# Order edges around the four token scatters of a sequence, with a landing wait for each of the four

## The chip, the cores and the metric

The kernel runs on one core of a Trainium2 chip. A core has five engines, each with its own instruction stream: TensorE (PE in the profile, with its weight loads as PEld), VectorE (DVE), ScalarE (ACT), GpSimd (POOL) and SyncE (SP), which here only starts DMAs. An engine takes its instructions in the order of its stream and waits on semaphores where one needs what another engine or a DMA has to deliver. The metric is the device time of one execution in microseconds (us), as a median over several runs; lower is better.

## The reference

Two transformer layers over 16 sequences of 512 tokens of width 128, each part followed by a layernorm:

```python
x = _layernorm(x + _L0_attn_ref(x, ...), axis=-1)   # prefix sums over the tokens, 16 heads
x = _layernorm(x + _L0_ffn_ref(x, ...), axis=-1)    # 8 experts, the best one of each token
x = _layernorm(x + _L1_attn_ref(x, ...), axis=-1)   # softmax attention with a position bias
x = _layernorm(x + _L1_ffn_ref(x, ...), axis=-1)    # a shared expert, and the best of 8
```

What matters here are the two mixtures. Each token goes through one expert of eight, picked by the largest logit:

```python
logits = tokens @ Wr + br
expert = jnp.argmax(jax.nn.softmax(logits, axis=-1), axis=-1)
...
out = jnp.take_along_axis(y, expert[:, None, None], axis=1)[:, 0, :]
```

## The kernel before

The sequences are handled in six chunks of 2, 3, 4, 4, 2 and 1 (`CHUNKS`, L31). Layer 0 of the next chunk is woven between the attention of layer 1 of the present one and the mixture of layer 1 of the chunk before, so that all engines have work of several kinds.

A mixture works on lists. `route` (L576) finds the expert of every token of the chunk and gives each token a row number, `place`, in a list in DRAM that is sorted by expert; each slot of 128 rows belongs to one expert, whose row numbers in the weight table are in `rows`. `scatter` (L694) then sends the tokens of one sequence to their rows with four indirect DMAs on GpSimd, one for each 128 tokens (`send`, L703). There are 32 such sequences in the two layers, so 128 scatters of 64 KB. `slots` (L743) reads the list back four slots at a time: SyncE fetches the tokens (`fetch_tokens`, L755, tile `xq`), GpSimd gathers the weights of each slot (`fetch`, L770, tile `ws`), TensorE transposes the tokens (`pts`, L783) and multiplies (`ph` L1012 in layer 0, `pg` and `pu` L1385 in layer 1, `py` L808), and the results go back to DRAM. `gather` (L721) fetches each token's result with four indirect DMAs per sequence (tile `yg`); its first waits for the last of the sequence before. All indirect DMAs have the line of the helper `indirect`, L678.

GpSimd has other work too: in the attention of layer 0 (`tile0`, L884) the product `self` (L913) and a DMA that adds one row, `carry`, to `ev` (L920), before the prefix sums `cum` (L929); two small instructions `rs` in every layernorm (L520, L521); the scaled tokens `xs_m` of layer 1's mixture (L1334). Around these stand on TensorE `pv` (L894), whose product with `ex` is `ev` on VectorE (L907), the sums `ce` (L845, L847), `po` (L952) and `y` (L960). In layer 1's attention `s` (L1127, L1134), its maxima `tops` (L1149), their transposes `pm` (L1162), `st` (L1190), `p` (L1205 and L1211) and `av` (L1220) follow one another; SyncE moves rows into `qk_pad` between them (L1111, L1175).

The order of all this is computed ahead. Every piece of work is an `op` with an engine, a cost, a delay, what it reads and writes, and a due time. `Plan.order` (L106) plays the engines through in time: on each engine the able op that is due first starts, if its buffers are free. The op of the four scatters has the cost 5.1 us on GpSimd and a delay of 2.5 us. The result is one list over all engines. The ops are emitted in that order, and at the end (L1589) every instruction gets an edge without a semaphore, "NoSync", to the one emitted before it. Such an edge only asks that the second is not placed before the first when the streams of the engines are laid out; on the chip nothing waits for it.

In `send`, a scatter has edges of two other kinds. `awaits` adds edges with a semaphore: to the DMA that clears the list and to the fetches that read the list two chunks ago. And since all scatters write one DRAM tensor, the framework would draw an edge with a semaphore from each to the earlier ones; for the second to fourth of a sequence `declare_no_dep` takes out the edges to every scatter of the chunk sent so far, and for the first it is not called.

Of the kernel before, what the change touches and what calls it, by code (L numbers as in the profile page):

```python
# [20 lines left out]
NT = N // P  # L21
# [47 lines left out]
class Plan:  # L69
# [8 lines left out]
    def op(self, engine, cost, emit, reads=(), writes=(), delay=None):  # L78
        if delay is None:
            delay = (0.25, 0.12, 0.15, 0.15, 3.4)[engine]  # L80
        o = Op(len(self.ops), self.due, engine, cost, delay, emit)
        self.ops.append(o)
        before = set()
        for k in reads:
            if k in self.last:
                before.add(self.last[k])
        for k in writes:
            if k in self.last:
                before.add(self.last[k])
            before.update(self.readers.get(k, ()))  # L90
        for k in reads:
            self.readers.setdefault(k, []).append(o)
        for k in writes:
            self.last[k], self.readers[k] = o, []
        before.discard(o)
        for b in before:
            b.then.append(o)
        o.waits = len(before)
        for k in (*reads, *writes):
            buf = k[0] if isinstance(k, tuple) else k  # L100
            if isinstance(buf, Buf) and buf not in o.bufs:
                o.bufs.append(buf)
                buf.left += 1
        return o
# [76 lines left out]
def block_kernel(ctx: ExitStack, tc: tile.TileContext, d, out: bass.AP):  # L181
    nc = tc.nc
# [43 lines left out]
    op = plan.op  # L226
    names, listed = {}, {}
    placed, fetched, zeroed, gathered = {}, {}, {}, {}

    def buf(kind, name):  # L230
        pool, shape, dtype, bufs = kinds[kind]
        return Buf(
            kind, lambda: pool.tile(shape, dtype, tag=kind, name=name, bufs=bufs)
        )
# [84 lines left out]
    def tok(ap):  # L319
        return ap.rearrange("p (t w) -> p t w", w=W)  # L320
# [356 lines left out]
    def indirect(out=None, to=None, in_=None, of=None):  # L677
        nc.gpsimd.indirect_dma_start(  # L678
            out, bass.IndirectOffsetOnAxis(to, 0) if to is not None else None,
            in_, bass.IndirectOffsetOnAxis(of, 0) if of is not None else None,  # L680
        )

    def last():
        return list(nc.cur_bb.bb.instructions)[-1]

    def awaits(inst, others):
        for other in others:
            tc.add_manual_dep(
                inst, other.name,
                mybir.DependencyInfo(mybir.DependencyClass.Sync, mybir.DependencyReason.DATA),  # L690
                reason="list of tokens",
            )

    def scatter(which, c, i, src, place, store):  # L694

        n = f"{which}_{c}"
        sent, taken = placed.setdefault(n, []), fetched.get(f"{which}_{c - 2}", [])
        before = [f"zeros{which}_{c % 2}"]  # L700
        before += [f"fetched{which}_{c - 2}_{s}" for s in range(0, SLOTS, 4)]

        def send():  # L703
            for t in range(NT):
                indirect(
                    out=store[0], to=place()[:, NT * i + t : NT * i + t + 1],
                    in_=tok(src())[:, t, :],
                )
                inst = last()
                if t:  # L710
                    for other in sent:
                        tc.declare_no_dep(inst, other, reason="rows of their own")
                awaits(inst, [zeroed[f"{which}_{c % 2}"], *taken])
                sent.append(inst)

        op(
            POOL, 5.1, send, reads=[src, place, *before, f"token{n}_{i - 1}"],
            writes=[f"token{n}_{i}"], delay=2.5,
        )
# [862 lines left out]
    order = plan.order()  # L1582
    block = nc.cur_bb.bb.instructions
    mark = len(block)
    for o in order:
        for made in o.makes:
            made.tile = made.make()
        o.emit()
    chain = [i for i in list(nc.cur_bb.bb.instructions)[mark:]]  # L1589
    for before, then in zip(chain, chain[1:]):  # L1590
        tc.add_manual_dep(
            then, before.name,
            mybir.DependencyInfo(mybir.DependencyClass.NoSync, mybir.DependencyReason.DATA),
            reason="order",
        )


# [84 lines left out]
```

## Time and profile before

| | |
|---|---|
| median of three runs | 2499.63 us (2495.47 to 2499.99) |
| the profiled execution, its own time | 2567.31 us |
| its span, first to last instruction | 2564.4 us |
| granted TensorE clock in it | 0.938 |
| scatters (`tokens`, L678) | 128, median 0.97 us each |
| gathers of weights and of results (L678) | 212 in 207.6 us, 128 in 126.4 us |

All durations below are those of the profiled execution, which took 2.7% longer than the median of the runs. A line of a timeline has the start and the duration in us, engine, line, operation and tiles (written<-read), and in brackets the idle time of the engine before it with what ended it. "issue" there means that the engine waited for nothing that the profile shows. A line of the waits has who waited, for whom, the total in us, how often, and the longest. A line of the chain has start, duration, engine, tile and line. For a DMA that GpSimd starts, the duration is the engine's part alone, not the transfer.

### The profile page before, as it was taken

The page shows a single profiled execution, that of the slowest core. Times are in us where ns is not written, and L with a number is a line of the kernel's source. Part 1 is how long each engine was busy: PE and PEld are TensorE (multiplying, and loading weights), DVE is VectorE, ACT ScalarE, POOL GpSimd, SP SyncE. Part 2 cuts the span into 40 slices and gives each one's busy share as a digit, 9 for nine tenths or more (in the row PEclk, how much of TensorE's full clock was granted, in tenths as well). Part 3 has the DMA queues.
Part 4 walks back from the last instruction along what each step waited for, and adds up shares of the span by engine and source line. Part 5 has one row for each costly group of instructions (what it writes and reads, how often), then busy time and mean ns, then how long its engine had stood idle before and what let it go on. Part 6 is the DMA issues. An engine that isn't in the chain of part 4 may idle for free.

```text
span 2564.4 us, 33958 instructions
## 1 busy us (share of the span) xinstructions
PE 2258.0 (88%) x12820; PEld 1125.6 (44%) x12820; DVE 1934.8 (75%) x3030; ACT 1000.6 (39%) x1336; POOL 731.2 (29%) x763
## 2 busy tenths in 40 slices
PE   5978889899997997899889988899999889998974
PEld 4556424344553443355434423454344235443443
DVE  5455787897786789777778798778887886789761
ACT  6323144533433543333335443334454333444330
POOL 1244322323223244312132343212213323223232
PEclk9999889999998998898989998999999899998886
DMA  7613113112011331211023411122223112332332
GB/s 179 196 37 101 29 51 90 42 32 75 16 44 52 99 99 30 62 54 41 10 55 102 113 39 46 40 68 70 54 63 90 52 41 74 113 104 62 90 102 88
DMA packets 152438, 179.96 MB, mean 70 GB/s; under 512 B 19332, under 2 KB 125444, under 8 KB 152276
## 3 DMA queue, kind: packets, MB, share of 16 engines
q1 hardware_dynamic: 125588, 84.27, 12.5%
q0 software_dynamic: 26688, 93.53, 12.2%
q8 instruction: 101, 1.65, 0.3%
q14 instruction: 61, 0.50, 0.1%
HBM read 127.67 MB, written 42.93 MB: 67 GB/s over the span
## 4 chain that ended last, share of the span: by engine, by line
PE 58%; DVE 26%; ACT 5%; issue 5%; DMA 2%; another core or an unknown queue 2%; POOL 1%; SPq 0%; DVEq 0%; POOLq 0%; ACTq 0%
PE st L1190 9%; DVE p L1205 9%; PE av L1220 7%; PE s L1127 5%; DVE tops L1149 5%; PE y L960 4%; PE cum L929 4%; PE pv L894 4%; PE s L1134 3%; PE py L808 3%; ACT p L1211 2%; PE po L952 2%; PE pg L1385 2%; DVE o L941 2%
## 5 line engine op out<-in xcount | busy, mean ns | idle before, releaser
L1211 ACT ACTIVATE p<-p 128x1024 f32<-128x1024 f32 x512 | 539.4, 1058 | 539.0 <-DVE p L1205 480.8
L1205 DVE TENSOR_TENSOR p<-st,bias 128x1024 f32<-128x1024 f32 x512 | 606.0, 1216 | 126.1 <-PE st L1190 95.7
L1149 DVE TENSOR_REDUCE tops<-s 128x2 f32<-128x1024 f32 x512 | 604.7, 1215 | 72.5 <-PE s L1134 48.2
L1190 PE MATMUL st<-qk_pad 32*128 32x512 f32 x2048 | 385.2, 663 | 35.6 <-DVE p L1205 20.6
L678 POOL DMA_INDIRECT ws<-tab,rows x212 | 207.6, 979 | 678.9 <-PE py L808 317.8
L1127 PE MATMUL s<-bias,ident 128*128 128x512 bf16 x1024 | 329.4, 403 | 64.0 <-DVE p L1205 37.1
L1220 PE MATMUL av<-p,vaug 128*32 128x512 f32 x2048 | 291.6, 641 | 21.2 <-ACT p L1211 18.2
L913 POOL TENSOR_TENSOR self<-ev,own 128x1024 f32<-128x1024 f32 x64 | 122.6, 1917 | 514.5 <-DVE ev L907 283.7
L1134 PE MATMUL s<-qk_pad 32*128 32x512 bf16 x1024 | 207.0, 397 | 4.1 <-DMA qk_pad<-qk 4.0
L1190 PEld LDWEIGHTS st<-qk_pad 32*128 32x128 f32 x2048 | 113.5, 189 | 190.2 <-issue 70.5
L1127 PEld LDWEIGHTS <-ident 128*128 128x128 bf16 x1024 | 82.3, 99 | 234.6 <-issue 226.4
L678 POOL DMA_INDIRECT yg<-results,place x128 | 126.4, 988 | 141.2 <-issue 46.0
L1134 PEld LDWEIGHTS <-qk_pad 32*128 32x128 bf16 x1024 | 48.8, 91 | 244.2 <-issue 232.9
L929 PE MATMUL cum<-ev,tri 128*128 128x512 f32 x256 | 133.1, 647 | 10.2 <-DVE p L1205 5.1
L960 PEld LDWEIGHTS y<-ow,ot 128*128 128x128 f32 x1024 | 125.6, 197 | 32.8 <-issue 15.2
L960 PE MATMUL y<-ow,ot 128*128 128x128 f32 x1024 | 131.3, 283 | 3.2 <-ACT ot L955 2.6
L894 PE MATMUL pv<-vw,xt 128*128 128x512 f32 x256 | 130.1, 634 | 3.7 <-DVE p L1205 1.9
L941 DVE TENSOR_TENSOR o<-cum,gg 128x1024 f32<-128x1024 f32 x64 | 78.2, 1222 | 68.0 <-PE cum L929 53.2
L808 PEld LDWEIGHTS py<-ws,h 128*128 128x128 f32 x848 | 101.8, 195 | 36.2 <-DVE h L1309 14.4
L907 DVE TENSOR_TENSOR ev<-pv,ex 128x1024 f32<-128x1024 f32 x64 | 78.0, 1220 | 51.6 <-PE pv L894 45.3
L808 PE MATMUL py<-ws,h 128*128 128x128 f32 x848 | 111.2, 285 | 6.3 <-DVE h L1309 5.3
L952 PE MATMUL po<-ident,o 128*128 128x128 f32 x512 | 72.0, 286 | 36.7 <-DVE o L945 30.8
(189 smaller groups left out, 2757.0 us busy)
## 6 DMA issues: line engine op xcount, KB each, us to landing
xq<-tokens SPq DMA_DIRECT2D x44, 256.0 KB
results<-yq SPq DMA_DIRECT2D x44, 256.0 KB
qk_pad<-qk SPq DMA_DIRECT2D x256, 32.0 KB
slid<-line SPq DMA_DIRECT2D x16, 448.0 KB
tokens<-zero SPq DMA_DIRECT2D x4, 1472.0 KB
xt<-in_xt SPq DMA_DIRECT2D x16, 256.0 KB
x<-in_x SPq DMA_DIRECT2D x16, 256.0 KB
qk_pad<-qk SPq DMA_DIRECT2D x256, 16.0 KB
```

The costliest lines, as they stand in the source:

```text
L678: nc.gpsimd.indirect_dma_start(out, bass.IndirectOffsetOnAxis(to, 0) if to is not None else None, in_, bass.IndirectOffsetOnAxis(of, 0) if ...
L808: nc.tensor.matmul(py()[:, col(s)], h()[:, c, col(s)], ws[s]()[:, off + c * W : off + (c + 1) * W], start=(c == 0), stop=(c == 1),)
L894: nc.tensor.matmul(pv()[:, hf, :], xt()[:, col(t)], vw[:, hf * N : (hf + 1) * N], start=True, stop=True,)
L929: nc.tensor.matmul(cum()[:, hf, :], tri, ev()[:, hf, :], start=True, stop=True)
L960: nc.tensor.matmul(y()[:, :P], ot()[:, hf, col(c)], ow[:, 4 * hf + c, :], start=(hf == 0 and c == 0), stop=(hf == 1 and c == 3),)
L1127: nc.tensor.matmul(s()[:, i, :], ident16, bias16[:, 4 * g + 2 * jp + i, 2 * u + 1 : 2 * (u + N) : 2], start=True, stop=False,)
L1134: nc.tensor.matmul(s()[:, i, :], pad[r, 0, col(it)], pad[r, 1, :], start=False, stop=True,)
L1149: lambda s=s, jp=jp: nc.vector.tensor_reduce(tops[g % 2][:, it, 2 * jp : 2 * jp + 2], s(), AX.X, ALU.max, negate=True,),
L1190: nc.tensor.matmul(s[jp]()[:, i, :], pad[r, 1, col(jt)], pad[r, 0, :], start=True, stop=True,)
L1205: lambda jp=jp, h=h, pj=pj: nc.vector.tensor_tensor(pj(), s[jp](), bias[:, h : h + 2, u : u + N], ALU.add),
L1211: ACT, 1.0, lambda pj=pj: nc.scalar.activation(pj(), pj(), AF.Exp),
L1220: nc.tensor.matmul(acc()[32 * j : 32 * j + 32, :], va[:, jt, h * VW : h * VW + 32], p[j // 2]()[:, j % 2, :], start=(jt == 0), stop=(jt == ...
```

## The change

In `send`, the four scatters of a sequence are kept in a list of their own, `row`. `declare_no_dep` is called only between members of one row. Each of the four gets an edge with a semaphore to the four of the sequence before in the same chunk's list, in place of what the first alone had. The row is noted in `together` under the name of each of its members. At the end, the list of instructions is turned into a list of rows: a scatter's row stands as one entry, every other instruction is an entry of its own. The NoSync edges go from all members of an entry to all members of the next; none is drawn inside a row. Costs, delays and due times stay as they are, and so does the list that `Plan.order` makes.

```diff
     placed, fetched, zeroed, gathered = {}, {}, {}, {}
+    together = {}
...
         def send():
+            before, row = sent[-NT:], []
             for t in range(NT):
                 indirect(
                     out=store[0], to=place()[:, NT * i + t : NT * i + t + 1],
                     in_=tok(src())[:, t, :],
                 )
                 inst = last()
-                if t:
-                    for other in sent:
-                        tc.declare_no_dep(inst, other, reason="rows of their own")
-                awaits(inst, [zeroed[f"{which}_{c % 2}"], *taken])
-                sent.append(inst)
+                for other in row:
+                    tc.declare_no_dep(inst, other, reason="rows of their own")
+                awaits(inst, [zeroed[f"{which}_{c % 2}"], *taken, *before])
+                row.append(inst)
+            sent.extend(row)
+            for inst in row:
+                together[inst.name] = row
...
-    chain = [i for i in list(nc.cur_bb.bb.instructions)[mark:]]
+    chain = []
+    for i in list(nc.cur_bb.bb.instructions)[mark:]:
+        row = together.get(i.name, [i])
+        if i is row[0] or i.name == row[0].name:
+            chain.append(row)
     for before, then in zip(chain, chain[1:]):
-        tc.add_manual_dep(
-            then, before.name,
-            mybir.DependencyInfo(mybir.DependencyClass.NoSync, mybir.DependencyReason.DATA),
-            reason="order",
-        )
+        for a in before:
+            for b in then:
+                tc.add_manual_dep(
+                    b, a.name,
+                    mybir.DependencyInfo(
+                        mybir.DependencyClass.NoSync, mybir.DependencyReason.DATA
+                    ),
+                    reason="order",
+                )
```

## The prediction

> **What bounds the kernel now.** I read the page first: busy shares and the chain that ended last. Then POOL's timeline around the scatters (the first columns are start and duration in us, the bracket is the idle time before and what ended it), then who waits for whom, then the chain in the stretches where scatters run.
>
> ```profile
> PE 2258.0 (88%) x12820; PEld 1125.6 (44%) x12820; DVE 1934.8 (75%) x3030; ACT 1000.6 (39%) x1336; POOL 731.2 (29%) x763
> PE 58%; DVE 26%; ACT 5%; issue 5%; DMA 2%; another core or an unknown queue 2%; POOL 1%; SPq 0%; DVEq 0%; POOLq 0%; ACTq 0%
> ```
>
> TensorE and VectorE hand the end to each other. POOL, which the change concerns, is busy 29% and holds 1% of the chain. So the question is what a move on POOL does to the other two.
>
> ```profile
> 186.42 0.97 POOL L678 DMA_INDIRECT tokens<-x,place  x1 [0.30 <-issue]
> 187.69 0.96 POOL L678 DMA_INDIRECT tokens<-x,place  x1 [0.30 <-issue]
> 188.96 0.96 POOL L678 DMA_INDIRECT tokens<-x,place  x1 [0.30 <-issue]
> 190.23 0.97 POOL L678 DMA_INDIRECT tokens<-x,place  x1 [0.30 <-issue]
> 191.22 1.91 POOL L913 TENSOR_TENSOR self<-ev,own 128x1024 f32<-128x1024 f32 x1
> 193.44 0.95 POOL L920 DMA_DIRECT2D ev<-carry  x1 [0.31 <-POOL self L913]
> 194.69 1.03 POOL L678 DMA_INDIRECT tokens<-x,place  x1 [0.30 <-issue]
> ...
> POOL tokens L678 <- issue: 36.8, 121, 0.3
> ```
>
> This is the first chunk, two sequences, eight scatters from 182.26 on. Seven run in a row, one each 1.27 us, then come the product for `self` and the row add, then the eighth. One `send` emits its four scatters together, and the planner's list puts `self` and the row add between the two sequences' fours. So this issue order is not the list's: the edges between the four siblings, for which `declare_no_dep` is also called, are not in force, and the list falls apart at every sequence. And no scatter waits for a landing: the longest such gap is 0.3 us, plain issue.
>
> What a landing wait costs POOL is shown by the row gathers of the combine step, where the first of a sequence waits for the landing of the sequence before:
>
> ```profile
> 2321.47 0.94 POOL L678 DMA_INDIRECT yg<-results,place  x1 [0.30 <-issue]
> 2324.20 0.94 POOL L678 DMA_INDIRECT yg<-results,place  x1 [1.79 <-DMA yg<-results,place]
> ...
> 2500.31 0.97 POOL L678 DMA_INDIRECT tokens<-xs_m,place  x1 [0.30 <-issue]
> ...
> 2502.57 0.37 SPq L756 DMA_DIRECT2D xq<-tokens  x1
> ```
>
> 1.79 us instead of 0.30. The last two lines give the scatter's own landing: SyncE's fetch of the listed tokens starts 2.26 us after the last scatter's start.
>
> What stands on POOL behind the bursts:
>
> ```profile
> 398.43 0.99 POOL L678 DMA_INDIRECT ws<-tab,rows  x1 [45.10 <-PE st L1190]
> 832.53 1.90 POOL L913 TENSOR_TENSOR self<-ev,own 128x1024 f32<-128x1024 f32 x1 [17.46 <-DVE ev L907]
> 1358.14 0.99 POOL L678 DMA_INDIRECT ws<-tab,rows  x1 [4.98 <-PE py L808]
> 1864.11 0.23 POOL L520 TENSOR_SCALAR rs<-mv 128x4 f32<-128x4 f32 x1 [15.51 <-DVE mv L515]
> 2418.45 0.97 POOL L678 DMA_INDIRECT ws<-tab,rows  x1 [23.32 <-PE py L808]
> ```
>
> POOL idles long after nearly every burst; the shortest cover is 4.98 us, at 1353.
>
> **What the Trainium skill says.** "DMA: Bandwidth & Descriptors", section "Anatomy of one DMA — SWDGE (gpsimd) path": about 2.0 us plus bytes/436e3 per DMA, most of it completion, and a semaphore wait is held by the issuing sequencer. For a 64 KB scatter that makes an estimate of 2.15 us; the trace's 2.26 agrees. "Perfetto Trace Analysis", section "DMA Instruction — SWDGE (GPSIMD)": the reported end is that of descriptor generation. The trace agrees: 0.97 us reported, 2.26 to the landing. The first page, section "Two DMAs through the same engine are not ordered", asks for a wait only where bytes are shared; the scatters write rows of their own, so the new waits protect nothing that the time depends on.
>
> **The change part by part.**
>
> 1. The landing waits. 32 sequences scatter (16 in each layer), in 12 chunk lists; the first of a list has nothing before it, so 20 fours get a wait. Only the first of a four pays: the other three find it ended. Price of one: 1.79 − 0.30 = 1.49 us from the gather; from the scatter's landing 2.26 − 0.97 − 0.30 = 0.99 us. I take 1.3. In the planner's list 5 of the 20 have enough POOL work between (`self` with the row add, four weight gathers, or the layernorm's `rs`), 2 have one `xs_m` product (1.03 us, 0.3 left), 13 are bare: 13 × 1.3 + 0.6 = 17.5 us of added POOL idle (13.5 to 20). At most two bare ones fall in one burst, 2.6 us, against the covers above (45, 17, 29, 15, 23 us). Charged to the end: 0.
>
> 2. The restored order on POOL. Where the list has `self` and the row add between two fours (first chunk at 187, layer-1 lists at 581 and 2111), they go back before three (or six) scatters: 3 × 1.27 = 3.8 us earlier, 7.6 at 2111. Nobody waited for them: in the first chunk the chain runs over other work (below), at 581 the row add issued at 587.23 is first needed by `cum` at 594.26, at 2125.74 `cum` follows PE work without a gap. Gain 0; if they were waited for, up to 3.8 + 3.8 + 7.6 = 15 us.
> Later go: in layer 0's second chunk of four (1326 to 1353) the list puts eight scatters behind `rs`, which waits to 1349.25 for VectorE; today only two are there. After `rs` at 1350.8 now come 8 × 1.27 + 1.3 = 11.5 us, so POOL is free at 1362.2, and the weight gather of 1358.14 starts 4.1 us late. Its last packets, now at 1367.5, come near 1371.6; `ph` starts at 1371.17 and needs the fourth tile 1.5 us later. So it just fits (loss 0 to 4). The last token lands at about 1363.1, and SyncE, issuing attention rows until 1364.3, reaches the fetch after that: 1.2 us of slack. In layer 0's first chunk of four (784 to 815) three scatters go behind the weight gathers: the fetch at 818.03 moves by 3.8 us, and SyncE's next order is not due before 830.79. Cost 0.
>
> 3. The restored order elsewhere. Comparing the list with the issue order, PE differs in 5 places, DVE and ACT in one each, SyncE nowhere. Two matter in the chain. At 188.98 `ce` runs before `pv` though `ev` waits for `pv`:
>
> ```profile
> 188.98 0.17 PE ce L845 x2
> 189.15 0.63 PE ce L847 x6
> 189.78 2.68 PE pv L894 x4
> 192.46 0.02 issue
> 192.48 1.24 DVE ev L907
> ```
>
> With `pv` first the 0.80 us of `ce` fall into PE's idle time before `cum`: −0.8. At 360.30 three transposes `pm` (0.73 us) stand before `st`, for which DVE waits 1.60 us: −0.7. The other three places exchange works of under 1 us with PE busy before and after: 0 ± 0.5 each.
>
> 4. More instructions: a few semaphore reads on POOL, 17 ns each, covered as in 1. Buffers and semaphores may be handed out in another order where the order differed; the trace can't show it. I bound it at 4 us either way, since nearly every pool is full there and has one buffer to give, and take 0.
>
> Sum: −0.8 − 0.7 = −1.5 us on the profiled execution, whose own time is 2567.3 (span 2564.4); the runs shown have a median of 2499.6, 2.6% below it, which takes nothing noticeable off 1.5. Forecast: 2498.
>
> **Rivals.**
> A, slower: the stretch 1350 to 1372 is not covered. For it: the chain there really passes the token fetch (5.14 us from 1364.63 until `pts`), and the weights then move beside it. It decides from the point where the last weight tile lands after 1372.7, or the last token after 1364.3. Price: 4.1 us for the weights and about 1.5 for the fetch: 2505. Against it: both fit on paper.
> B, faster: `self` and the row add were late today, and what follows them moves up by the 15 us of part 2; half of that gives 2492, all of it 2485. Against it: the chain doesn't pass POOL in these places.
> C, it doesn't do what it says: the list is still not kept, only waits are added. Then part 1 alone, covered: 2499.6.
> All 17.5 us of waits on the path would give 2517; the covers speak against it, and I leave it outside.
>
> **How the numbers follow.** Likeliest 2498 with 0.48, its own range 2494 to 2503 from the 4 us of part 4. A 0.25, B 0.20, C 0.07. What can be told from no change is 0.2%, 5.0 us: 2494.6 to 2504.6. A and its neighbours give slower 0.25; B gives faster 0.22; the rest, same 0.53. The range reaches from B's half to beyond A by the 4 us of part 4: 2488 to 2509.
>
> **What would show it.** Four scatters of one sequence adjacent on POOL, `self` between the fours in the first chunk; 13 gaps of about 1.6 us (0.3 + 1.3) released by the DMA of `tokens`; POOL's busy time unchanged; `pv` before `ce` at 189; no new waits of `pts` or `ph`. I am wrong if the gaps are over 4 us, if `ph` near 1371 waits for `ws`, if SyncE's wait at the token fetch grows in front of attention rows, or if the time moves while these places do not.

## The result and the profile after

The changed kernel takes 2495.77 us (median of 20 runs, 2488.25 to 2503.71), the kernel before beside it 2501.77 (20 runs, 2495.47 to 2516.98). The ratio is 0.9972 with a 95% interval of 0.9959 to 0.9985: 0.28% less, some 7 us (the medians stand 6.0 apart). The forecast was 2498 and "no change"; the time lies in the range, and the gain is just above what can be told from none.

The profiled execution of after has 2503.2 us (span 2501.2). That of before had 2567.3 (span 2564.4), although the three runs listed with it took 2495 to 2500 and none of the twenty here more than 2517. So the two profiles stand 64 us apart where the runs stand 6 apart. Part of this document is about those 58 us, since the prediction read its places in the longer profile.

First the page of after, busy time and chain of waits:

```profile
PE 2242.6 (90%) x12820; PEld 1122.7 (45%) x12820; DVE 1936.2 (77%) x3030; ACT 1000.9 (40%) x1336; POOL 734.1 (29%) x763
...
PE 60%; DVE 25%; ACT 5%; issue 4%; DMA 3%; POOL 2%; SPq 0%; DVEq 0%; POOLq 0%; ACTq 0%
```

TensorE has 15 us less busy time for the same 12820 products (at a mean granted clock of 0.942 against 0.938), and the 2% of "another core or an unknown queue" are gone from the chain. GpSimd (POOL) does the same work as before, 734.1 us against 731.2.

GpSimd's timeline of after in the first chunk, with one landing wait of a later list (start and duration in us, in brackets the idle time before and what ended it), and its waits (total, times, longest):

```profile
187.14 1.02 POOL L679 DMA_INDIRECT tokens<-x,place  x1 [0.31 <-issue]
188.46 1.46 POOL L679 DMA_INDIRECT tokens<-x,place  x1 [0.30 <-issue]
190.22 0.97 POOL L679 DMA_INDIRECT tokens<-x,place  x1 [0.30 <-issue]
191.50 0.97 POOL L679 DMA_INDIRECT tokens<-x,place  x1 [0.30 <-issue]
192.48 1.92 POOL L917 TENSOR_TENSOR self<-ev,own 128x1024 f32<-128x1024 f32 x1
194.70 0.95 POOL L924 DMA_DIRECT2D ev<-carry  x1 [0.30 <-POOL self L917]
195.95 1.03 POOL L679 DMA_INDIRECT tokens<-x,place  x1 [0.30 <-issue]
...
347.37 0.97 POOL L679 DMA_INDIRECT tokens<-x,place  x1 [0.30 <-issue]
350.46 0.97 POOL L679 DMA_INDIRECT tokens<-x,place  x1 [2.12 <-DMA tokens<-x,place]
```

```profile
POOL tokens L679 <- issue: 37.0, 107, 2.5
...
POOL tokens L679 <- DMA tokens<-xs_m,place: 13.9, 10, 2.3
POOL tokens L679 <- DMA tokens<-x,place: 13.1, 6, 3.2
```

The change did what it says. The fours are adjacent, and `self` and the row add stand between two of them. The two named groups hold 16 idle times, 27.0 us in all, but three of these are the ordinary 0.3 us that stands in front of any scatter. The 13 others last 2.0 us on average, and two more, of 2.1 and 2.5 us, stand under "issue". So 15 scatters pause for a landing, 2.05 us each, where the prediction had 13 of 1.6. In front of all 128 scatters GpSimd idles 118.0 us, whatever it waits for, against 91.5 before.

### The profile page after: what moved, and what is told of

The parts are those of the page before. It is cut to its first block, busy times and chain, and to the rows that moved or that the text cites. A ratio compares the mean times of both kernels' runs of the same rounds, so it can differ in the third digit from the quotient of the medians.

```text
span 2501.2 us, 33949 instructions
## 1 busy us (share of the span) xinstructions
PE 2242.6 (90%) x12820; PEld 1122.7 (45%) x12820; DVE 1936.2 (77%) x3030; ACT 1000.9 (40%) x1336; POOL 734.1 (29%) x763
## 4 chain that ended last, share of the span: by engine, by line
PE 60%; DVE 25%; ACT 5%; issue 4%; DMA 3%; POOL 2%; SPq 0%; DVEq 0%; POOLq 0%; ACTq 0%
PE st L1194 9%; DVE p L1209 8%; PE av L1224 7%; PE s L1131 6%; DVE tops L1153 5%; PE y L964 4%; PE pv L898 4%; PE py L812 4%; PE cum L933 4%; PE s L1138 3%; PE po L956 2%; ACT p L1215 2%; PE pg L1389 2%; DVE o L945 2%; PE ph L1016 2%
## 5 line engine op out<-in xcount | busy, mean ns | idle before, releaser
L1194 PE MATMUL st<-qk_pad 32*128 32x512 f32 x2048 | 378.0, 662 | 25.2 <-DVE p L1209 20.7
```

Source lines behind the costliest of these rows:

```text
L1194: nc.tensor.matmul(s[jp]()[:, i, :], pad[r, 1, col(jt)], pad[r, 0, :], start=True, stop=True,)
```

## The experiments

They ran in three groups, each on a chip of its own with the kernel before beside it: e1 to e4 where before took 2572.3 us, e5 to e8 where it took 2502.2, e9 to e12 where it took 2504.2. That the same kernel takes 70 us more on one chip turned out to be half of the answer.

### Taking the change apart: e1 to e4

**e1** is the kernel before and **e4** the changed kernel, both unedited. **e2** has the changed edges and order without the landing waits:

```diff
-                for other in row:
+                for other in [*sent, *row]:
                     tc.declare_no_dep(inst, other, reason="rows of their own")
-                awaits(inst, [zeroed[f"{which}_{c % 2}"], *taken, *before])
+                awaits(inst, [zeroed[f"{which}_{c % 2}"], *taken])
```

**e3** has the waits without the order: the chain of before, and each scatter waits for the preceding four:

```diff
+            before, row = sent[-NT:], []
...
-                if t:
-                    for other in sent:
-                        tc.declare_no_dep(inst, other, reason="rows of their own")
-                awaits(inst, [zeroed[f"{which}_{c % 2}"], *taken])
-                sent.append(inst)
+                for other in row:
+                    tc.declare_no_dep(inst, other, reason="rows of their own")
+                awaits(inst, [zeroed[f"{which}_{c % 2}"], *taken, *before])
+                row.append(inst)
+            sent.extend(row)
```

TensorE, VectorE and ScalarE issue in e3 as in before. GpSimd differs at two places: once `rs`, and at the list of 2111 `self` with the row add, go out ahead of three scatters that stand before them in e1.

> The kernel before, unchanged. Theory N (the profiled execution of before was an odd one): a profile near the runs' median, 2495 to 2517 us, and VectorE's idle gaps in the scatter bursts (8.3 us at 804, 4.1 at 1039, 5.0 at 1346, 4.7 at 1595) are gone. Theory S (long runs of scatters that nothing holds back stall TensorE): the same gaps at the same places again, a profile several us above that of the changed kernel. Ratio 1.000 +- 0.001 in both.

> The changed kernel's issue order on all engines, but no scatter waits for the landing of an earlier one. Theory O (the restored order is what gains: pv before ce, st before the transposes, self earlier): the whole gain, ratio 0.997, VectorE's gaps in the bursts gone. Theory S (the landing waits gain, since they break the runs of scatters): no gain, 0.999 to 1.001, and gaps of 3 to 8 us at 800, 1040, 1345 and 1600 stay.

> The landing waits of the change, with the edges between neighbours as before: PE, DVE, ACT and SP keep the order of before, and three of four scatters of the next sequence still stand ahead of the last of the present one. Theory O: no gain, 0.999 to 1.001. Theory S: the gain, ratio 0.997 to 0.998, gaps in the bursts gone.

> The changed kernel, unchanged. All theories: ratio 0.996 to 0.9985, no gap of VectorE over 3 us in the bursts at 800, 1040, 1345 and 1600.

Measured against before on that chip: e1 0.9996 (0.9975 to 1.0016), e2 0.9935 (0.9910 to 0.9960), e3 0.9785 (0.9767 to 0.9803), e4 0.9801 (0.9779 to 0.9822). Here the change is worth 2%, and the waits, which the prediction priced as a cost to be hidden, bring all of it alone. Theory N falls, since before's profile comes out at 2573.5 again. The sizes were missed: e3 and e4 gain several times what was expected of them, and the order alone (e2) brings a third of the whole, more than theory O gave it and more than the nothing of theory S.

Where the time went is seen at one burst. GpSimd, TensorE and VectorE in e1, with the burst whose scatters begin at 1041.30 ("remote" is a releaser that the profile cannot name):

```profile
1048.99 0.96 POOL L678 DMA_INDIRECT tokens<-xs_m,place  x1 [0.30 <-issue]
1050.26 0.97 POOL L678 DMA_INDIRECT tokens<-xs_m,place  x1 [0.30 <-issue]
...
1047.67 0.62 PE L1127 MATMUL s<-bias,ident 128*128 128x512 bf16 x2
1048.23 0.39 PE L1134 MATMUL s<-qk_pad 32*128 32x512 bf16 x2
1048.55 1.06 PE L1220 MATMUL av<-p,vaug 128*32 128x512 f32 x8
1051.04 1.13 PE L1190 MATMUL st<-qk_pad 32*128 32x512 f32 x4 [1.42 <-issue]
1055.24 2.08 PE L1190 MATMUL st<-qk_pad 32*128 32x512 f32 x4 [3.08 <-issue]
...
1049.76 1.23 DVE L1149 TENSOR_REDUCE tops<-s 128x2 f32<-128x1024 f32 x1 [4.15 <-PE av L1220]
1053.96 1.22 DVE L1149 TENSOR_REDUCE tops<-s 128x2 f32<-128x1024 f32 x1 [2.98 <-remote]
1057.46 1.23 DVE L1149 TENSOR_REDUCE tops<-s 128x2 f32<-128x1024 f32 x1 [2.28 <-PE st L1190]
```

The same three reductions in e3:

```profile
1019.17 3.49 DVE L1150 TENSOR_REDUCE tops<-s 128x2 f32<-128x1024 f32 x3 [2.08 <-PE s L1135]
```

In e1 the last of the three `s` tiles was sent by TensorE at 1048.23, yet VectorE gets them at 1049.76, 1053.96 and 1057.46, one in four microseconds; TensorE in turn waits for what VectorE should have done, with gaps that the profile can only call "issue". TensorE's signals for these three tiles, which the trace keeps, are late as well: 1049.73, 1053.94 and 1057.44, where e9 (below), the same kernel on another chip, has 1016.09, 1017.01 and 1017.89. So the delay lies with TensorE or its signal, not with VectorE. In e3 the three follow each other without a gap. The row of granted clock has a dip to 0.5 for 10.2 us from 1052.78 on in e1 and none there in e3. It begins 3 us after the first late tile, so it does not start the stall; how much of the later delay it carries was not tried.

Matching VectorE's instructions of e1 one by one with those of e3 gives what each run of GpSimd's issues lost, from its start to 8 us after its end. The last column is the same between e9 and e10, that is on a chip where before takes 2504 us:

| run in e1, from | indirect transfers in a row | lost on e3 | e9 on e10 |
|---|---|---|---|
| 343.8 | 12 | 8.5 us | 1.1 us |
| 790.6 | 15 | 8.6 | −0.3 |
| 1036.1 | 16 | 8.9 | 0.1 |
| 1335.7 | 14 | 5.3 | −0.6 |
| 1590.3 | 15 | 9.7 | 0.0 |
| 2113.7 | 14 | 4.5 | 2.0 |
| 2392.1 | 12 | 2.6 | 2.8 |
| 37 runs of four weight gathers, sum | 4 each | −0.9 | 5.5 |

These seven hold 48 of the 61 us. The last two are weak evidence, since e9 loses 2 to 3 us on e10 there as well. Length alone does not decide it either: of two runs of eleven in e1 one loses nothing (from 181.8) and one 2.2 us (from 577.1), and one of eight (from 1851.1) loses 5.7. A check comes from the changed kernel. In e4 it still has one run of twelve, from 790.84 on, where four weight gathers follow four scatters and the next four follow these without a pause. Matched with e12, the same kernel on another chip, it loses 11.2 us there and at most 3.3 in any of its runs of eight. VectorE in e4, behind that run's start:

```profile
798.25 1.23 DVE L1153 TENSOR_REDUCE tops<-s 128x2 f32<-128x1024 f32 x1 [3.66 <-issue]
...
808.32 1.22 DVE L1209 TENSOR_TENSOR p<-st,bias 128x1024 f32<-128x1024 f32 x1 [6.03 <-remote]
```

These are gaps over 3 us, which were expected to be gone in e4. e3 has no run longer than eight.

So on this chip a run of a dozen and more indirect transfers, one each 1.27 us, can stall TensorE, in the burst shown from some 8 us after its first scatter on, and pauses of about 2 us between the fours prevent it. Theory S holds for this chip, as far as it names runs and pauses; its "no gain" for the order alone does not. The order shortens some runs too (the fourteen from 1335.7 on are two of eight in e2), so the gain of e2 is not clear of the stall.

### Pauses without waits, waits without pauses: e5 to e8

e5 fills a spare tile instead of waiting, e6 waits for landings long past, e7 waits in twos, and e8 is a measurement by itself. Against e2, the changed kernel, and the changed kernel:

```diff
+            for _ in before[:3]:
+                nc.gpsimd.memset(spare, 0.0)
             for t in range(NT):
```

```diff
-            before, row = sent[-NT:], []
+            before, row = sent[-2 * NT : -NT], []
...
-                for other in row:
+                for other in [*sent[-NT:], *row]:
```

```diff
-            before, row = sent[-NT:], []
+            before, row = sent[-2:], []
...
-                for other in row:
+                pair = row[t // 2 * 2 :]
+                if t == 2:
+                    before = row[:2]
+                for other in pair:
```

The core of e8, and its five parts:

```python
        for step in range(STEPS):
            s = ps.tile([P, N], F32, tag="s", name="s")
            nc.tensor.matmul(s, ident16, x16, start=True, stop=False)
            nc.tensor.matmul(s, ident16, x16, start=False, stop=True)
...
    parts = [
        lambda: send(0, False, False), lambda: send(1, True, False),
        lambda: send(2, False, True), fills, lambda: send(3, False, False),
    ]
```

> The order of the change without its landing waits, as in e2; instead GpSimd fills a spare tile three times (0.7 us each, some 2.1 us together) before each four that would have waited for the four before it: 60 fills, no scatter waits for a landing. The scatters are then broken up in fours as in the changed kernel, by work and not by a wait. Theory S, that a long run of scatters issued back to back stalls TensorE and that any pause of about 2 us ends it: the gain of the changed kernel comes back, a ratio of 0.978 to 0.984 where the changed kernel had 0.980 and order alone 0.9935; VectorE's gaps of 3 to 8 us in front of `tops`, `p` and `h` in the scatter stretches are gone. Rival W, that the wait for the landing itself is what helps (GpSimd idle, or the data in memory): no more than order alone, 0.991 to 0.996, with the gaps still there. Rival F, that GpSimd's fills slow VectorE: over 0.996.

> The changed kernel, but each four waits for the landing of the four before the preceding one, so for scatters issued 5 to 8 places earlier. At 1.27 us for an issue and 2.2 us to land these have landed when their turn comes, so the waits are there and are met, and scatters still go out back to back. Theory S: nothing of the landing waits' gain is left, the ratio is that of order alone, 0.991 to 0.996, the group `tokens <- DMA tokens` is under 3 us, and VectorE's gaps are those of e2. Rival W, that it is the waits as such (semaphores read, fewer scatters outstanding than the queue allows): 0.978 to 0.984.

> The changed kernel, but in twos: each two scatters wait for the landing of the two before them, so the pauses are more than twice as many (some 48 instead of 20, 80 to 100 us of GpSimd idle instead of 27) and no run is longer than two. Theory S: fours were short enough already, nothing more is gained, and the longer scatter stretches are mostly covered: 0.978 to 0.985. Rival G, that the stall grows from the first scatters on and fours still pay some of it: below 0.976. Rival C, that the longer stretches hold up `rs`, `self` and the weight gathers: over 0.987.

> The computation is left out: TensorE makes the same 128x512 tile from two bf16 products 720 times, VectorE reduces each one, and nothing on these two depends on GpSimd. Beside that GpSimd does five things, each begun on a result of VectorE 120 tiles after the last: 24 scatters of 128 rows of 512 bytes back to back; 24 where each four waits for the landing of the four before; 24 with three fills of a spare tile between fours; 48 fills; and 24 back to back again. Theory S: the tiles run at a steady pace of 0.6 to 0.9 us except in the first and the fifth part, where from 8 to 10 us after the first scatter on VectorE waits 2 to 5 us for a tile, until the run ends; the other three parts keep the pace. Rival K, that the stall needs something else of this kernel (weight gathers on the same queue, transfers of SyncE, transposes): the pace is the same in all five parts. Rival B, that any GpSimd work beside TensorE does it: the part with fills is slow too.

Measured: e5 0.9980 (0.9967 to 0.9994), e6 0.9941 (0.9921 to 0.9961), e7 1.0062 (1.0046 to 1.0078). The expectations were written for a chip like the first. On this one the stall does not occur: matched with the profile of after, e6 loses at most 1.6 us in any of its unbroken runs of 8 to 16. So e5 and e6 leave open whether a pause filled with work would have done as well as a wait. What they show is the other side, the price of pauses where nothing is won by them: none in e6, 15 in the changed kernel (0.9972), 20 filled ones in e5, and in e7 these:

```profile
POOL tokens L679 <- issue: 66.0, 93, 3.7
...
POOL tokens L679 <- DMA tokens<-xs_m,place: 35.2, 16, 3.8
POOL tokens L679 <- DMA tokens<-x,place: 26.9, 13, 2.6
```

In front of the scatters of e7 GpSimd idles 182 us, against 118 in the changed kernel and 91 in before. That costs e7 0.9% against the changed kernel and 1.2% against e6, which ran on the same chip: rival C of that run. The intervals of e5 and e6 do not meet either, so the filled pauses cost something there. Fours are affordable, twos are not.

e8, of which there is one execution, is level. Its page, VectorE's group (busy time and mean ns, then idle time in front) and the row of the granted clock:

```profile
PEclk9999999999999999999999999999999999999999
...
L261 DVE TENSOR_REDUCE top<-s 128x4 f32<-128x512 f32 x720 | 431.1, 672 | 1.9 <-PE s L259 1.8
```

720 tiles and 1.9 us of idle time in all, 24 scatters back to back or not. As the stall is absent on this chip from the whole kernel too, that does not say what else it needs.

### Where nothing stalls: e9 to e12

**e9** is before and **e12** the changed kernel, unedited, **e10** is the kernel of e3. **e11** restores the order of everything but the scatters: a second chain of edges runs past them, so TensorE, VectorE and ScalarE issue as in the changed kernel and GpSimd as in before.

```diff
+                row.add(inst.name)
...
-    for before, then in zip(chain, chain[1:]):
+    rest = [i for i in chain if i.name not in row]
+    for before, then in [*zip(chain, chain[1:]), *zip(rest, rest[1:])]:
```

> The kernel before once more, unchanged, for its profile: the profiled executions of before so far (2567.3 us, and e1 with 2575.3) both belong to the slow kind, while 41 timed executions beside e5 to e7 had a median of 2502.2. Theory T, two kinds of chips (or of places of the program in memory): where the times beside it are near 2500, the profiled span is near 2500 too, the long runs of scatters are there all the same, and VectorE's gaps of 3 to 8 us in front of `tops`, `p` and `h` behind them are missing; where the times are near 2570 the gaps are there. Rival: the profiler makes them, so that a profile near 2565 comes with times near 2500. Ratio 0.998 to 1.002.

> The neighbour edges of before, so its order on TensorE, VectorE and ScalarE, with each scatter waiting for the landing of the four before, as in e3. Theory T on a chip where before takes about 2500 us: no stall is there to be broken up, so the pauses can only cost: 1.000 to 1.006 (e6 without pauses stood at 0.9941, the changed kernel with 27 us of pauses at 0.9972, e7 with over 60 us at 1.0062, so about 0.003 for 27 us). Where before takes about 2570 us: 0.977 to 0.981, as in e3. Rival: the pauses cost nothing and e6, after and e7 differ for another reason: 0.998 to 1.000.

> No landing waits; the scatters stay where before has them, loose between each other, and GpSimd's whole order is that of before. Edges past the scatters hold the other instructions in the order written out, so TensorE (52 positions), VectorE (2) and ScalarE (3) issue as in the changed kernel. It splits part 3 of the prediction from part 2. Theory P, that the gain of order alone (0.9941 in e6, 0.9935 in e2) is TensorE's restored order: 0.992 to 0.996. Rival G, that it is GpSimd's restored order (the self term, the row addition and the weight gathers no longer pushed back by scatters): 0.998 to 1.001. The prediction's own sizes, 0 for GpSimd's order and 1.5 us for TensorE's, would give 0.9994.

> The changed kernel again, unchanged, on the chip of e9 to e11, so that the four add up: (order of the rest) and (GpSimd's order) and (waits). Where before takes about 2500 us: 0.996 to 0.999. Where it takes about 2570: 0.978 to 0.982.

Measured: e9 0.9989 (0.9973 to 1.0005), e10 0.9990 (0.9972 to 1.0009), e11 0.9978 (0.9967 to 0.9988), e12 0.9963 (0.9942 to 0.9985). The profile of e9 has a span of 2502.5 us, so the profiler does not make the 60 us on this chip. T holds: the stall belongs to the chip, or to something that differs between loads on it, and not to the program alone. e10 lies where its rival had it (the pauses cost nothing), e11 between its two theories. GpSimd in e9 issues runs as long as in e1 (the table above), and in the same burst as shown of e1 (here its sixteen issues go from 1004.7 to 1024.9) VectorE gets its three tiles like this:

```profile
1016.11 3.48 DVE L1149 TENSOR_REDUCE tops<-s 128x2 f32<-128x1024 f32 x3 [1.92 <-PE s L1134]
1020.08 1.23 DVE L1205 TENSOR_TENSOR p<-st,bias 128x1024 f32<-128x1024 f32 x1 [0.48 <-PE st L1190]
```

One more thing sets the profiles apart, and it tells which kind the one shown of before is. The traces keep the signals by which DMAs report that they have landed. There are 12487 of them in before and 12415 to 12905 in e1 to e4, but 16866 to 16949 in after, e5 to e7 and e9 to e12. A scatter has nearly all of its 16 in e9, and in e1 on average 5.9 in layer 0 and 3.8 in layer 1. So the profile shown of before has the mark of the chip of e1 to e4. Whether these signals are only missing from the record, or are held up on the chip together with TensorE, the runs do not tell.

The clean profile of before also shows what the order did. GpSimd, TensorE and VectorE in e9, then in e12, in the last layer-1 list:

```profile
2059.76 0.97 POOL L678 DMA_INDIRECT tokens<-xs_m,place  x1 [0.30 <-issue]
2060.76 1.91 POOL L913 TENSOR_TENSOR self<-ev,own 128x1024 f32<-128x1024 f32 x1
2062.97 0.95 POOL L920 DMA_DIRECT2D ev<-carry  x1 [0.30 <-POOL self L913]
...
2065.17 1.95 PE L929 MATMUL cum<-ev,tri 128*128 128x512 f32 x4 [2.83 <-DMA ev<-carry]
...
2067.16 1.22 DVE L941 TENSOR_TENSOR o<-cum,gg 128x1024 f32<-128x1024 f32 x1 [3.33 <-PE cum L929]
```

```profile
2053.07 1.91 POOL L917 TENSOR_TENSOR self<-ev,own 128x1024 f32<-128x1024 f32 x1
2055.28 0.95 POOL L924 DMA_DIRECT2D ev<-carry  x1 [0.30 <-POOL self L917]
...
2062.25 1.98 PE L933 MATMUL cum<-ev,tri 128*128 128x512 f32 x4
...
2064.27 1.23 DVE L945 TENSOR_TENSOR o<-cum,gg 128x1024 f32<-128x1024 f32 x1 [0.47 <-PE cum L933]
```

The two profiles stand at the same time here to within 0.1 us. In e9 the row add stands behind ten scatters and TensorE's cumulative sum waits 2.83 us for it. In e12 it goes out 7.7 us earlier, the wait is gone, and VectorE gets `cum` 2.9 us earlier. In e11, where GpSimd keeps the order of before, VectorE's gap at this place is 6.50 us.

And here is what the order and the waits cost, at the place of rival A. TensorE in e9, then in e12:

```profile
1329.61 0.66 PE L783 MATMUL pts<-ident,xq 128*128 128x128 f32 x4 [1.66 <-DMA xq<-tokens]
...
1331.56 3.00 PE L1012 MATMUL ph<-xqt,ws 128*128 128x128 f32 x16
...
1336.56 2.05 PE L808 MATMUL py<-ws,h 128*128 128x128 f32 x16
```

```profile
1330.69 1.12 PE L787 MATMUL pts<-ident,xq 128*128 128x128 f32 x4 [2.79 <-DMA xq<-tokens]
...
1333.13 3.78 PE L1016 MATMUL ph<-xqt,ws 128*128 128x128 f32 x16
...
1338.95 2.05 PE L812 MATMUL py<-ws,h 128*128 128x128 f32 x16
```

The last scatter in front starts at 1320.61 instead of 1311.92, `pts` comes 1.1 us later, `ph` 1.6 and `py` 2.4. What is late is the token fetch; whether the later scatters or the weight transfers beside it hold it up was not separated.

## Why the prediction came out as it did

The time was right and the account of it half right: what came was not the likeliest case, no change, but a small gain. Rival B's mechanism made a part of it and rival A's took most of that part back. That the measured median lies 2.2 us from 2498 is luck: the gain was −1.5 in the forecast and −7.0 in the runs, and before stood 2.1 us higher in the comparison than in the three runs that the forecast started from. Point by point:

**Part 1, the landing waits, charged to the end with 0.** On the chips of the result and of e9 to e12 nothing speaks against it. The size was wrong: predicted were 17.5 us of added idle time (13.5 to 20), measured are 118.0 − 91.5 = 26.5. A pause of 2.05 us is 1.75 over the ordinary 0.3, not 1.3. The reading of the scatter's own landing (0.99) took the next scatter to start as soon as the last one lands, 2.26 us after its start; after the change it starts 3.1 us after it (347.37 to 350.46). The larger cost was covered all the same: e10 adds 38 us of idle time and stands at 0.9990 with 1 inside its interval, where e9, without any, has 0.9989. The step that failed is the one before it, that a wait on GpSimd can only be a cost. On the chip of e1 to e4 the same waits bring 2%. The profile shown of before has the same pattern, and its signs were there: a span 65 us above the runs' median, which the prediction noted and passed over ("which takes nothing noticeable off 1.5"), the 2% of an unknown releaser in the chain, and `tops` waiting 4.13 us for TensorE inside one burst and `h` 8.33 us for ScalarE just behind another. VectorE at this `h`, in the profile shown of before and then in e9:

```profile
804.23 1.22 DVE L1302 SCALAR_TENSOR_TENSOR h<-h,pg 128x1024 f32<-128x1024 f32 x1 [8.33 <-ACT h L1297]
...
781.76 1.22 DVE L1302 SCALAR_TENSOR_TENSOR h<-h,pg 128x1024 f32<-128x1024 f32 x1 [1.55 <-ACT h L1297]
```

On such a chip the forecast would have been off by 47 us (2572.3 − 1.5 against the 2524.3 of e4).

**Part 2, GpSimd's order, "nobody waited for them", gain 0.** Wrong in one place of three: at the list of 2111 in the profile shown, where the row add moves by 7.6 us as predicted (7.7 measured), it is waited for, and 2.9 us are won. The prediction concluded from "`cum` follows PE work without a gap" at 2125.74; but that TensorE was late for another reason, the stall. In the undisturbed profile there is a gap of 2.83 us. In all, e9 has only 3.6 us of TensorE waiting for this row add, so the 15 us of rival B were never to be had. The other half of part 2, "it just fits (loss 0 to 4)", came out inside its bounds: the weight gather goes out 4.6 us later (4.1 predicted), `ph` starts 1.6 us later and `py` 2.4. The 1.2 us of slack that the token fetch was given are not there: the sign named for it, new waits of `pts`, appears (10.4 us in three waits in e12, 8.4 in two in e9). So the loss takes most of the 2.9 us back.

**Part 3, TensorE's order, −1.5 us.** Probably too small. e11 has this and nothing else, and is 0.0012 to 0.0033 faster, 3 to 8 us; but e9, which is before itself, stands at 0.9989 in the same group, so some of that may be chance. The first of its two places came out as predicted: in e9 `ce` stands before `pv`, and from the start of `y` to `cum` there are 194.78 − 188.80 = 5.98 us; in e12 `pv` comes first and it is 195.10 − 189.81 = 5.29, 0.7 saved where 0.8 was said. Where the rest of e11's gain comes from I could not find: single executions of one kernel differ by 5 us before the first changed instruction, and no place after it stands out in all of them. The places found in parts 2 and 3 come to 2.9 − 2.4 + 0.7 = 1.2 us, so most of the 7 us is not located.

**Part 4, other effects, 0 ± 4.** Nothing in the runs speaks against it; part 3's missing microseconds may be here.

The sum was −1.5 and is −7.0 (3.8 to 10.3). That the gain comes from the order and not from the waits is shown where nothing stalls: order without pauses stands at 0.9941 (e6), waits without the order at 0.9990 (e10). With both it is 0.9972 and 0.9963. The intervals of e6 and of these touch, and e10 shows no cost, so that the waits give back some 0.3% of the order's gain there is possible and not shown. The range held because A and B were both in it; that "same" got 0.53 rested on taking part 3 at two places and part 2 at nothing.

What stays open is why TensorE stalls on one chip and not on two others. That runs of transfers issued without a pause set it off there, and that waits end it, is shown by e1 to e4; that the pause is what helps, and not the landing, or that fewer transfers are outstanding, was not tried on such a chip. Nor was the recording itself: the stall and the missing records of landings come on the same chip, every run on record lists its span and its clock, and no run tells whether the kernel would stall there with nothing recorded. No version beats the others on both: e6 has the best ratio where nothing stalls, e3 where it does, and the changed kernel is near the best in both.

## What to carry to other kernels

When a profile's own time stands 2.6% off the runs' median, settle that first: places read from it may belong to a disturbance, and a gap that is missing in it (TensorE late, so nobody waits for the row add) can be as misleading as one that is there. A wait on an engine that idles 70% is not only a cost: on one chip a pause after every four scatters was worth 1.3% on top of the restored order and 2.1% without it, on others it cost nothing that these runs can tell, at most some 0.3%, and pauses after every two cost 0.9% more there. An order written out by hand is worth checking in the issue order of each engine, because edges removed between siblings let other engines' instructions slip too: restoring them was worth 0.2% here, and 0.6% with GpSimd's own order (e6, on another chip).

## What the runs showed of the hardware

Beyond the stall, one thing was not expected. In the first chunk the restored order lets GpSimd's `self` product start earlier, and it meets a scaling on VectorE; VectorE and then GpSimd in e12:

```profile
189.98 2.35 DVE L318 TENSOR_SCALAR ex<-ex 128x192 f32<-128x192 f32 x1
...
190.30 1.91 POOL L917 TENSOR_TENSOR self<-ev,own 128x1024 f32<-128x1024 f32 x1
```

The scaling takes 0.26 us in e9, where no product of GpSimd runs beside it, and 2.35 here, until 0.12 us after that product's end; in the profile of after it is 2.36 and again ends 0.13 us after. The Trainium skill has this on the page "SBUF — State Buffer", section "SBUF: two separate sides": GpSimd and some VectorE forms share a pair of ports, held by one for a whole instruction while the other blocks. The trace agrees that the scaling is held until the product ends, with these numbers; which of the two took the ports first it does not show, as the scaling's record begins 0.32 us before the product's. It cost little here, some 0.2 us, since the `ev` behind it waits 2.32 us for TensorE in e9 anyway, but it is a price of moving a GpSimd product that the prediction did not count.
